# Layer 1 of a two-layer convolution kernel: splines in two partition halves, x1 loaded 64 partitions at a time, output stores ahead of loads

## The chip, the cores and the metric

The kernel runs on one core of a Trainium2 chip. The metric is device time in microseconds (us), the median over runs of the whole kernel. Names of engines: PE is the matrix engine, DVE the vector engine, ACT the scalar engine, POOL the GpSimd engine, SP the engine that issues most of the DMAs.

## What is computed

The input x has 4 images of 16 channels, 256 by 256, in float32. Two layers follow each other, each with a group normalization in front and a residual sum behind:

```python
x = x + L0(group_norm(x))     # 3x3 conv to 16*25 logits, softmax over 25,
                              # weighted sum over the 5x5 neighbourhood
x = x + L1(group_norm(x))     # a KAN convolution, 3x3 neighbourhood
```

The reference adds a third thing to know about layer 1, and it is all that the change touches:

```python
patches = extract_patches(x, k=3, padding=1)
base_w = base_weight.sum(axis=2)
spl_w = (spline_weight * spline_scaler[..., None]).sum(axis=2)
out = einsum('bjhwn,ijn->bihw', silu(patches), base_w)
out = out + einsum('bjhwns,ijns->bihw', b_splines(patches, grid), spl_w)
out = out + bias
```

There are 8 cubic spline bases for each of 16 channels, so 128 spline features of a pixel, one per partition, and beside them the silu of each channel. A padded pixel is zero after normalization: its silu is zero, its splines are those of zero. The residual x of layer 1 is also fed through the matmuls, as an identity weight on the unnormalized x1 rows.

## The kernel before, in words

Layer 0 walks over strips of 32 columns. It writes its result x1 to DRAM buffers `x1s[b]`, one per image, from a store that ACT issues (the very last one POOL issues). Its statistics give, per image, the scale and bias that layer 1 needs (`scales`, L174 on). In the profile layer 0 lasts until about 2039 us, with DVE's reductions at L738 and POOL's products at L906.

Layer 1 walks over 64 units (4 images, 16 units each), a unit being 16 output rows. For unit n:

- `load_x(n, half)` (L984 to L991, the DMA is L988): the unit's x1 rows go to one of three buffers xta, xtb, xtc, each channel repeated over 8 partitions, in two DMAs of 128 partitions by 8 rows (1 MB each).
- `load_tiles(n)` (L995 to L1006, the DMAs are L1003): the same rows once more, 16 channels by 4 row phases d, into the upper 64 partitions of one of three sl buffers, a DMA of 16 neighbouring partitions for each d (128 KB each). Rows outside the image are zeroed by POOL (L999).
- `features(n, between)` (L1025): ACT takes the distance to the knots (L1036, an Abs with scale and bias per partition) over both halves; then for each half (buffers ta, tb) `spline` (L161 to L172) runs ACT steps L164, L166, L167 and DVE steps L168, L169, L170, which write 128 spline rows to the ring. For the second half DVE's `minus_r` (L159) stands in for L166. Between the halves `put` runs: DVE's L1065 adds the bias to the finished psum of unit n-2 and so makes yo.
- `silu(n)` (L1015, the ACT step is L1018) turns the sl rows to silu in the lower 64 partitions; POOL zeroes the outside rows again (L1023).
- `halo(n)`: at image edges POOL copies a pad row into the ring (L1053, L1057); every third unit SP copies two ring rows to the ring's start (L1055).
- `store()` (L1072): two DMAs write yo of unit n-2 to the output.
- `outputs(n)`: PE multiplies the ring rows (L1082) and the sl rows (L1092) by the weights, 48 and 12 matmuls in the program.

Every engine's instructions in layer 1 keep the order of the program text, SP's DMA issues among them; this order is laid down by hand (`in_order`). The loop body (L1127 to L1143) is therefore also SP's queue: halo's copy, then the two x loads of unit n+2, then the two stores of unit n-2, then the four tile loads of unit n+1. A load waits for the last reader of its buffer; a store waits for yo.

The weights are prepared once at the start: `prepare1` (L534) sums the spline weights into `wt` and places the base weights in `ws`; `sel` (L103, L104) spreads a value per channel over 8 partitions each; partition p of the splines stands for channel p // 8 and base p % 8. In `scales`, q holds the silu scale and bias (by p % 16) and the distance scale and bias (by p // 8).

Of the kernel before, what the change touches and what calls it, by code (L numbers as in the profile page):

```python
# [4 lines left out]

# [7 lines left out]
F32 = mybir.dt.float32  # L13
F32R = mybir.dt.float32r
AF = mybir.ActivationFunctionType
# [20 lines left out]
def conv_preact_kernel(  # L36
# [12 lines left out]
    nc = tc.nc  # L49
# [26 lines left out]
    RD = RT + 2  # L76
    RU = 16
    NU = H // RU
    SROWS = (0, 1, 3, 2)
    LAG1 = 2  # L80

    const = ctx.enter_context(tc.tile_pool(name="const", bufs=1))
# [11 lines left out]
    mhalf = const.tile([P, G], F32, name="mhalf")  # L94
    nc.vector.memset(mhalf, -0.5)
    ub = const.tile([P, 1], F32, name="ub")
    ubrow = const.tile([1, C, NS], F32, name="ubrow")
    for s in range(NS):
        nc.vector.memset(ubrow[:, :, s : s + 1], 3.5 - s)
    ident = const.tile([P, P], F32, name="ident")  # L100
    make_identity(nc, ident)

    sel = const.tile([C, C, NS], F32, name="sel")  # L103
    nc.vector.tensor_copy(sel, ident[0:C, 0:C].unsqueeze(2).to_broadcast([C, C, NS]))  # L104
    onec = const.tile([P, 1], F32, name="onec")
    nc.vector.memset(onec, 1.0)
    flag = const.tile([1, 1], mybir.dt.int32, name="flag")
# [15 lines left out]
    ws = const.tile([P, 3, RT, C], F32, name="ws")  # L123
    nc.gpsimd.memset(ws, 0.0)
    for r in range(RT):
        p = P // 2 + SROWS.index(r + 1) * C
        nc.sync.dma_start(ws[p : p + C, 1, r], ident[p : p + C, p : p + C])

    edge = const.tile([P, 5], F32, name="edge")
    stat1 = ctx.enter_context(tc.tile_pool(name="stat1", bufs=1))  # L130
# [43 lines left out]
    def scales(b, psum):  # L174


        def small(n, name):
            return stat1.tile([P, n], F32, name=f"{name}_{b}", tag=f"{name}{b % 2}")

        sums, d, mz, p = small(2 * G, "sums"), small(G, "d"), small(G, "mz"), small(G, "p")  # L180
        q = stat1.tile([P, 6], F32, name=f"q_{b}", tag=f"q{b}")
        nc.vector.tensor_reduce(sums, st1[b].rearrange("p t g k -> p (t g) k"), AX.X, ALU.add)
        yield
        ps = psum()[:, 0 : 2 * G]
        nc.tensor.matmul(ps, lhsT=ones, rhs=sums, start=True, stop=True)
        yield
        part = 1.0 / (GC * CX * NK)
        nc.scalar.activation(d, ps[:, 0:G], AF.Square, scale=part)
        yield

        nc.vector.scalar_tensor_tensor(mz, ps[:, 0:G], part, nrm[b][:, 1], ALU.mult, ALU.subtract)
        nc.vector.scalar_tensor_tensor(d, ps[:, G : 2 * G], part, d, ALU.mult, ALU.subtract)  # L192
        yield
        nc.gpsimd.tensor_add(d, d, nrz[b][:, 1])  # L194
        nc.gpsimd.tensor_tensor(p, d, mhalf, ALU.pow)
        nc.gpsimd.tensor_mul(d, p, nrz[b][:, 0])
        nc.gpsimd.tensor_mul(p, p, gsel_sb)
        nc.gpsimd.tensor_mul(p, p, mz)
        yield
        nc.vector.reduce_sum(q[:, 0:1], d, AX.X)  # L200
        nc.vector.reduce_sum(q[:, 1:2], p, AX.X)
        nc.vector.tensor_scalar(q[:, 1:2], q[:, 1:2], -1.0, None, ALU.mult)
        for k in range(2):
            nc.vector.tensor_scalar(q[:, 2 + k : 3 + k], q[:, k : k + 1], 2.5, None, ALU.mult)
        yield
        ps = psum()[:, 0:2]
        nc.tensor.matmul(
            ps, lhsT=sel.rearrange("p c s -> p (c s)"), rhs=q[0:C, 2:4], start=True, stop=True
        )
        yield  # L210
        nc.vector.tensor_copy(q[:, 4:5], ps[:, 0:1])
        nc.vector.tensor_add(q[:, 5:6], ps[:, 1:2], ub)
        sc[b] = tuple(q[:, k : k + 1] for k in (0, 1, 4, 5))
        yield

    sc = {}
# [31 lines left out]
    def zeros(b, queue):  # L248

        for e in (0, HP - PAD):  # L250
            for r in range(PAD):
                yield partial(
                    queue.dma_start,
                    hs[b][:, e + r].rearrange("s c w -> c s w"),
                    zero[0:C, 0 : NST * SP].rearrange("c (s w) -> c s w", s=NST),
                )
        for h in range(NH):
            for w in (0, (W + 1) * RP):
                yield partial(queue.dma_start, hst[b][h][:, w : w + RP], zero[0:C, 0:RP])
                yield partial(  # L260
                    queue.dma_start,
                    hsl[b][h][:, :, w : w + RP].rearrange("c t r -> (c t) r"), zero[:, 0:RP],
                )
# [178 lines left out]
    with tc.tile_pool(name="prep0", bufs=2) as prep, tc.tile_pool(  # L442
# [42 lines left out]
        for d in range(3):  # L485
# [10 lines left out]

        ups = pstat.tile([P, 1], F32, name="ups", tag="hps")
        nc.tensor.matmul(
            ups, lhsT=ubrow.rearrange("p c s -> p (c s)"), rhs=onec[0:1], start=True, stop=True
        )  # L500
        nc.vector.tensor_copy(ub, ups)
        nc.scalar.activation(edge[:, 0:1], ub, AF.Abs)
# [31 lines left out]
        def prepare1():  # L534

            nc.gpsimd.tensor_mul(sw, sw, ss)
            wc = pre.tile([P, 3, nm], F32, name="wc")
            for d in range(3):
                nc.vector.tensor_reduce(
                    wc[:, d], sw[:, d].rearrange("p k j -> p j k"), AX.X, ALU.add  # L540
                )
            nc.vector.tensor_scalar(wc, wc, -1.0 / 6.0, None, ALU.mult)
            wb1 = pre.tile([nm, nm], F32, name="wb1")
            nc.vector.tensor_reduce(wb1, bw.rearrange("p k j -> p j k"), AX.X, ALU.add)
            for r in range(RT):
                nc.vector.tensor_copy(
                    wt[:, r : r + 3, :, r, :], wc.rearrange("p d (e o) -> p d e o", e=3)
                )
                for d in range(3):
                    p = SROWS.index(r + d) * C  # L550
                    nc.sync.dma_start(
                        ws[p : p + C, :, r, :],
                        wb1[d * C : (d + 1) * C].rearrange("p (e o) -> p e o", e=3),
                    )

# [102 lines left out]
    def layer0(shift):  # L658
# [4 lines left out]
        with tc.tile_pool(name=f"prep{arm}", bufs=2) as prep, tc.tile_pool(  # L663
# [150 lines left out]
            def store(n, xc):  # L814
                b, hf, s = strips[n]
                c0 = s * SW + SW - CX
                v = x1s[b][:, 0 : H * W].rearrange("c (p w) -> p c w", w=W)

                queue = nc.gpsimd if n == len(strips) - 1 else nc.scalar
                queue.dma_start(v[hf * P : (hf + 1) * P, :, c0 : c0 + CX], xc)  # L820
# [110 lines left out]
    def layer1(arm, last, marks, seeds):  # L931
# [5 lines left out]
        with ExitStack() as pools:  # L937
# [27 lines left out]
            def rows(t, dims, r):  # L965

                return bass.AP(tensor=t.tensor, offset=t.offset + r * W, ap=dims)
# [16 lines left out]
            def load_x(n, half):  # L984
                b, u = units[n]
                lo, hs = halves(u)
                a, z = hs[half]
                nc.sync.dma_start(  # L988
                    xtt[n % 3][:, a - lo : z - lo, :],
                    rows(x1s[b], [[CP, C], [0, NS], [1, (z - a) * W]], u * RU - 1 + a),  # L990
                )  # L991

            def load_tiles(n):  # L995
                b, u = units[n]
                t = sl[n % 3][P // 2 :, :, 1 : W + 1]
                for p, q in outside(u):
                    nc.gpsimd.memset(t[p : p + C, q], 0.0)  # L999
                for k, d in enumerate(SROWS):  # L1000
                    q0 = 1 if (u, d) == (0, 0) else 0
                    q1 = RU // RT - (1 if (u, d) == (NU - 1, RD - 1) else 0)
                    nc.sync.dma_start(  # L1003
                        t[k * C : (k + 1) * C, q0:q1, :],
                        rows(x1s[b], [[CP, C], [RT * W, q1 - q0], [1, W]], u * RU - 1 + d + q0 * RT),
                    )  # L1006

            def outside(u):

                return [  # L1010
                    (SROWS.index(d) * C, q)
                    for at, d, q in ((0, 0, 0), (NU - 1, RD - 1, RU // RT - 1)) if u == at
                ]

            def silu(n):  # L1015
                b, u = units[n]
                t = sl[n % 3][0 : P // 2, :, 1 : W + 1]
                nc.scalar.activation(  # L1018
                    t, sl[n % 3][P // 2 :, :, 1 : W + 1], AF.Silu,
                    scale=sc[b][0][P // 2 :], bias=sc[b][1][P // 2 :],  # L1020
                )
                for p, q in outside(u):
                    nc.gpsimd.memset(t[p : p + C, q], 0.0)  # L1023

            def features(n, between):  # L1025
                b, u = units[n]
# [49 lines left out]
            def outputs(n):  # L1076
# [11 lines left out]

                for e in range(3):
                    for t in range(NT):  # L1090
                        v = slice(0, P if e == 1 else P // 2)
                        nc.tensor.matmul(  # L1092
                            yp[t * M : (t + 1) * M],
                            lhsT=ws[v, e].rearrange("p r o -> p (r o)"),
                            rhs=sl[n % 3][v, t : t + NT + 1 : NT, e : e + W],
                            start=False, stop=e == 2,
                        )
                waiting.append((b, u, yp))
# [28 lines left out]
            for n in range(len(units)):  # L1127
                if n % 2:
                    next(more, None)
                if n > 0:  # L1130
                    features(n, put)
                    silu(n)
                    halo(n)
                if n + 2 < len(units):
                    for half in range(2):
                        load_x(n + 2, half)
                store()
                if 0 < n < len(units) - 1:
                    load_tiles(n + 1)
                outputs(n)  # L1140
# [66 lines left out]
```

## Time and profile before

| | us |
|---|---|
| median of 3 runs | 3053.68 |
| the runs | 3051.6 to 3059.32 |
| span of the profiled execution, first to last instruction | 3050.8 |
| DVE busy over the span | 2954.8 (97%) |
| PE busy over the span | 2804.2 (92%) |
| ACT busy over the span | 2252.1 (74%) |
| POOL busy over the span | 1948.5 (64%) |

The three runs are times of the device for the whole kernel; the profiled execution is one more, whose span alone is shown. The busy shares are means over both layers, and the two layers use the engines differently: POOL and PE carry layer 0 along with DVE, while in layer 1 POOL is nearly idle and ACT is full. So layer 1 has to be read from stretches of time after 2087 us. Idle times "before" an instruction are listed with what ended them; the chain of waits follows the end of the program back to what released each step.

### The profile page before, as it was taken

How to read it: one execution, taken by the hardware profiler on the slowest of the kernel's cores; microseconds unless marked ns; L12 is line 12 of the kernel's file. 1: busy time of each engine (PE TensorE's matmuls, PEld its weight loads, DVE VectorE, ACT ScalarE, POOL GpSimd, SP SyncE). 2: the span in 40 equal slices, each digit the busy share in tenths (PEclk: the TensorE clock that was granted, in tenths of full speed). 3: DMA queues.
4: the chain of work that ended last, by engine and by line, in shares of the span. 5: the costliest groups of instructions: out<-in, count | busy, mean ns of one | idle time of the engine just before them, and what ended most of it. 6: DMA issues, size and time to landing. Idle time of an engine off the chain costs nothing.

```text
span 3050.8 us, 39867 instructions
## 1 busy us (share of the span) xinstructions
PE 2804.2 (92%) x14280; PEld 1447.6 (47%) x14280; DVE 2954.8 (97%) x1587; ACT 2252.1 (74%) x2619; POOL 1948.5 (64%) x744
## 2 busy tenths in 40 slices
PE   4699999999989999999999999958999999999998
PEld 3465656656656666666666556632222222222222
DVE  7599999999999999999999999999999999999997
ACT  6566776576765666766645646559999999999996
POOL 4399999999999999999999999980100100000000
PEclk7799999999999999999999999979999999999999
DMA  8988988878978778878857667659999999999993
GB/s 274 254 232 223 261 238 238 230 196 247 244 207 229 201 207 226 241 209 228 234 152 194 179 165 191 162 128 208 201 192 195 195 195 190 199 195 199 192 199 86
DMA packets 353042, 628.40 MB, mean 206 GB/s; under 512 B 41394, under 2 KB 218788, under 8 KB 336964
## 3 DMA queue, kind: packets, MB, share of 16 engines
q1 hardware_dynamic: 320132, 607.39, 81.0%
q10 hardware_dynamic: 30960, 15.73, 1.7%
q8 instruction: 117, 1.92, 0.3%
q0 software_dynamic: 1744, 2.64, 0.3%
q14 instruction: 89, 0.73, 0.1%
HBM read 516.05 MB, written 104.24 MB: 203 GB/s over the span
## 4 chain that ended last, share of the span: by engine, by line
DVE 68%; issue 12%; PE 9%; DMA 5%; ACT 3%; POOL 2%; SPq 1%; DVEq 0%; POOLq 0%; ACTq 0%
DVE nd L738 43%; PE lg L878 6%; DVE ta L169 4%; DVE ta L168 4%; DVE tb L169 4%; DVE tb L168 4%; DVE tb L159 2%; PE lg L882 2%; DVE yo L1065 1%; POOL e L906 1%; DVE r L759 1%; DMA an<-hsl 1%; DVE nd L758 1%; DVE nd L760 1%; DVE lo L396 1%
## 5 line engine op out<-in xcount | busy, mean ns | idle before, releaser
L906 POOL TENSOR_TENSOR e<-e,u 128x1600 f32<-128x1600 f32 x512 | 1788.5, 3543 | 56.4 <-ACT e L901 49.0
L878 PE MATMUL lg<-wm,am 128*128 128x400 f32 x4096 | 1735.7, 505 | 80.3 <-ACT e L901 49.1
L738 DVE TENSOR_REDUCE nd<-e 128x128 f32<-128x3200 f32 x512 | 1749.2, 3478 | 24.3 <-POOL e L906 24.3
L882 PE MATMUL lg<-wn,an 97*128 97x400 f32 x2048 | 1344.3, 656 | 12.8 <-DMA an<-hsl 12.7
L901 ACT ACTIVATE e<-lg 128x800 f32<-128x800 f32 x1024 | 820.0, 837 | 682.8 <-DVE nd L738 440.7
L878 PEld LDWEIGHTS lg<-wm,am 128*128 128x128 f32 x4096 | 759.9, 192 | 400.1 <-ACT e L901 104.5
L1082 PE MATMUL yp<-ring,wt 128*32 128x512 f32 x6144 | 745.3, 597 | 86.6 <-DVE ring L170 62.6
L882 PEld LDWEIGHTS lg<-wn,an 97*128 97x128 f32 x2048 | 388.1, 190 | 330.7 <-issue 21.7
L1082 PEld LDWEIGHTS yp<-ring,wt 128*32 128x32 f32 x6144 | 202.2, 109 | 621.6 <-issue 433.1
L999 POOL MEMSET sl<- 16x256 f32 x6 | 1.8, 306 | 402.9 <-PE yp L1092 396.8
L169 DVE TENSOR_TENSOR ta<-ta,ta 128x2048 f32<-128x2048 f32 (+1 forms) x64 | 147.4, 2303 | 3.0 <-ACT ta L167 2.9
L170 DVE SCALAR_TENSOR_TENSOR ring<-ta,ta 128x2048 f32<-128x2048 f32 (+1 forms) x64 | 147.8, 2310 | 2.5
L786 ACT ACTIVATE z<-xc,nrm 128x256 f32<-128x256 f32 x240 | 144.2, 601 | 6.4 <-POOL xc L766 2.4
L170 DVE SCALAR_TENSOR_TENSOR ring<-tb,tb 128x2048 f32<-128x2048 f32 x64 | 145.6, 2275 | 2.5
L169 DVE TENSOR_TENSOR tb<-tb,tb 128x2048 f32<-128x2048 f32 x64 | 145.2, 2269 | 0.0
L1092 PE MATMUL yp<-sl,ws 64*32 64x512 f32 (+1 forms) x1032 | 131.2, 602 | 0.0
L999 POOL MEMSET slc<- 16x256 f32 x2 | 0.6, 309 | 203.1 <-PE yp L1092 203.0
L167 ACT ACTIVATE ta<-ta 128x2048 f32<-128x2048 f32 (+1 forms) x64 | 123.4, 1928 | 2.0
L194 POOL TENSOR_TENSOR d<-d,nrz 128x8 f32<-128x8 f32 x4 | 2.7, 680 | 189.9 <-DVE d L192 189.9
L167 ACT ACTIVATE tb<-tb 128x2048 f32<-128x2048 f32 x64 | 120.6, 1884 | 0.0
L1018 ACT ACTIVATE sl<-sl,q 64x2048 f32<-64x2048 f32 x43 | 90.0, 2094 | 1.2
L766 POOL TENSOR_TENSOR xc<-xc,nd 128x512 f32<-128x512 f32 x64 | 82.8, 1293 | 8.3 <-DVE nd L760 8.3
(200 smaller groups left out, 2108.8 us busy)
## 6 DMA issues: line engine op xcount, KB each, us to landing
am<-hst SPq DMA_DIRECT2D x512, 194.6 KB
u<-hs SPq DMA_DIRECT2D x320, 288.0 KB
an<-hsl SPq DMA_DIRECT2D x512, 129.8 KB
xta<-x1s SPq DMA_DIRECT2D x40, 1024.0 KB
xtb<-x1s SPq DMA_DIRECT2D x40, 1024.0 KB
xtc<-x1s SPq DMA_DIRECT2D x40, 1024.0 KB
am<-hst SPq DMA_DIRECT2D x256, 129.8 KB
sl<-x1s SPq DMA_DIRECT2D x166, 128.0 KB
```

The source lines that it names most:

```text
L167: nc.scalar.activation(s1, r1, AF.Square, scale=2.0)
L168: nc.vector.scalar_tensor_tensor(s2, t, 2.0, s2, ALU.subtract, ALU.mult)
L169: nc.vector.tensor_mul(s1, s1, r1)
L170: nc.vector.scalar_tensor_tensor(f, s2, 0.0, s1, ALU.min, ALU.subtract if given else ALU.add)
L738: nc.vector.tensor_reduce(nd[:, :, :, j : j + JG].rearrange("p t c j -> p t j c"), e.rearrange("p t j m c d -> p t j c m d"), AX.XY, ALU.add,)
L786: nc.scalar.activation(z, v, f, scale=nrm[b][:, 0, g : g + 1], bias=nrm[b][:, 1, g : g + 1], accum_out=st1[b][:, t, g, columns_of(n) : col ...
L878: nc.tensor.matmul(lg[:, i, :NL], lhsT=am[:, o : o + P], rhs=wm.rearrange("p m c d -> p (m c d)"), start=True, stop=False,)
L882: nc.tensor.matmul(lg[:, i, :NL], lhsT=an[:, o : o + P], rhs=wn.rearrange("p m c d -> p (m c d)"), start=False, stop=True,)
L901: nc.scalar.activation(ev, lg[:, :, :NL], AF.Exp)
L906: nc.gpsimd.tensor_tensor(e[:, 1].rearrange("p j m c d -> p j (m c) d"), e[:, 0].rearrange("p j m c d -> p j (m c) d"), uv, ALU.mult,)
L1082: nc.tensor.matmul(yp[t * M : (t + 1) * M], lhsT=wt[:, d, e].rearrange("p r o -> p (r o)"), rhs=ring[:, r0 + t * RT + d : r0 + t * RT + d ...
L1092: nc.tensor.matmul(yp[t * M : (t + 1) * M], lhsT=ws[v, e].rearrange("p r o -> p (r o)"), rhs=sl[n % 3][v, t : t + NT + 1 : NT, e : e + W], ...
```

## The change

In layer 1 and what feeds it:

- Splines are placed in two partition halves: partition is now half, channel, base within the half (h, c, s with 4 bases each), instead of channel, base. `sel`, `ubrow` and the spline weights (through one matmul with a permutation, `order`) follow.
- `load_x` issues each of its two loads as two DMAs of 64 partitions.
- `load_tiles` puts row phase d of channel c at partition 64 + 4c + d, so one DMA writes every fourth partition of 64. `ws` follows. The scale and bias for silu now come from the same spread as the distance's.
- x1s gets a row of zeros ahead of and behind each image, written by one more DMA per image with the other zeros; tile rows outside the image are then loaded as zeros. POOL's memsets go. To make silu of such a row zero, boundary units run silu in two pieces, the outside row with scale and bias multiplied by zero (`inside`).
- PE's silu matmuls use all 128 partitions for all three column shifts.
- In the loop, `store()` stands ahead of the x loads.

```diff
-    sel = const.tile([C, C, NS], F32, name="sel")
-    nc.vector.tensor_copy(sel, ident[0:C, 0:C].unsqueeze(2).to_broadcast([C, C, NS]))
+    sel = const.tile([C, 2, C, SH], F32, name="sel")
+    for h in range(2):
+        nc.vector.tensor_copy(sel[:, h], ident[0:C, 0:C].unsqueeze(2).to_broadcast([C, C, SH]))
+
+    inside = const.tile([P, 2], F32, name="inside")
+    for k, d in enumerate((0, RD - 1)):
+        nc.vector.reduce_sum(inside[:, k : k + 1], ident[:, d:P:RD], AX.X)
+    nc.vector.tensor_scalar(inside, inside, -1.0, 1.0, ALU.mult, ALU.add)
...
-        nc.vector.tensor_copy(q[:, 4:5], ps[:, 0:1])
-        nc.vector.tensor_add(q[:, 5:6], ps[:, 1:2], ub)
-        sc[b] = tuple(q[:, k : k + 1] for k in (0, 1, 4, 5))
+        nc.vector.tensor_copy(q[:, 4:7], ps[:, 0:3])
+        nc.vector.tensor_add(q[:, 7:8], ps[:, 3:4], ub)
+        for k in range(2):
+            nc.vector.tensor_scalar(
+                q[:, 8 + 2 * k : 10 + 2 * k], ps[:, 0:2], inside[:, k : k + 1], None, ALU.mult
+            )
+        sc[b] = tuple(q[:, k : k + 1] for k in range(4, 12))
...
+        yield partial(
+            queue.dma_start,
+            bass.AP(
+                tensor=x1s[b].tensor, offset=x1s[b].offset,
+                ap=[[CP, C], [(H + 1) * W, 2], [1, W]],
+            ),
+            zero[0 : 2 * C, 0:W],
+        )
...
+            order = pre.tile([P, 2, C, SH], F32, name="order")
+            nc.vector.tensor_copy(order, ident.rearrange("p (c h s) -> p h c s", h=2, s=SH))
+            wcp = ptr0.tile([P, QG, P], F32, name="wcp", tag="tp").rearrange("p g w -> p (g w)")
+            wcp = wcp[:, 0 : 3 * nm]
+            nc.tensor.matmul(
+                wcp, lhsT=order.rearrange("p h c s -> p (h c s)"),
+                rhs=wc.rearrange("p d j -> p (d j)"), start=True, stop=True,
+            )
...
                 a, z = hs[half]
-                nc.sync.dma_start(
-                    xtt[n % 3][:, a - lo : z - lo, :],
-                    rows(x1s[b], [[CP, C], [0, NS], [1, (z - a) * W]], u * RU - 1 + a),
-                )
+                for h in range(2):
+                    nc.sync.dma_start(
+                        xtt[n % 3][h * P // 2 : (h + 1) * P // 2, a - lo : z - lo, :],
+                        rows(x1s[b], [[CP, C], [0, SH], [1, (z - a) * W]], u * RU + a),
+                    )
...
-                t = sl[n % 3][P // 2 :, :, 1 : W + 1]
-                for p, q in outside(u):
-                    nc.gpsimd.memset(t[p : p + C, q], 0.0)
-                for k, d in enumerate(SROWS):
-                    q0 = 1 if (u, d) == (0, 0) else 0
-                    q1 = RU // RT - (1 if (u, d) == (NU - 1, RD - 1) else 0)
+                for d in range(RD):
                     nc.sync.dma_start(
-                        t[k * C : (k + 1) * C, q0:q1, :],
-                        rows(x1s[b], [[CP, C], [RT * W, q1 - q0], [1, W]], u * RU - 1 + d + q0 * RT),
+                        sl[n % 3][P // 2 + d : P : RD, :, 1 : W + 1],
+                        rows(x1s[b], [[CP, C], [RT * W, RU // RT], [1, W]], u * RU + d),
                     )
...
-                t = sl[n % 3][0 : P // 2, :, 1 : W + 1]
-                nc.scalar.activation(
-                    t, sl[n % 3][P // 2 :, :, 1 : W + 1], AF.Silu,
-                    scale=sc[b][0][P // 2 :], bias=sc[b][1][P // 2 :],
-                )
-                for p, q in outside(u):
-                    nc.gpsimd.memset(t[p : p + C, q], 0.0)
+                q0, q1 = 1 if u == 0 else 0, RU // RT - (1 if u == NU - 1 else 0)
+                for a, z, k in ((0, q0, 4), (q0, q1, 0), (q1, RU // RT, 6)):
+                    if a < z:
+                        nc.scalar.activation(
+                            sl[n % 3][0 : P // 2, a:z, 1 : W + 1],
+                            sl[n % 3][P // 2 :, a:z, 1 : W + 1], AF.Silu,
+                            scale=sc[b][k][P // 2 :], bias=sc[b][k + 1][P // 2 :],
+                        )
...
                     for t in range(NT):
-                        v = slice(0, P if e == 1 else P // 2)
                         nc.tensor.matmul(
                             yp[t * M : (t + 1) * M],
-                            lhsT=ws[v, e].rearrange("p r o -> p (r o)"),
-                            rhs=sl[n % 3][v, t : t + NT + 1 : NT, e : e + W],
+                            lhsT=ws[:, e].rearrange("p r o -> p (r o)"),
+                            rhs=sl[n % 3][:, t : t + NT + 1 : NT, e : e + W],
                             start=False, stop=e == 2,
                         )
...
+                store()
                 if n + 2 < len(units):
                     for half in range(2):
                         load_x(n + 2, half)
-                store()
                 if 0 < n < len(units) - 1:
                     load_tiles(n + 1)
```

More of the change, by code (lines that the diff above doesn't have):

```diff
@@ L2 @@
 from functools import partial
-from itertools import chain
 from itertools import chain
@@ L78, in conv_preact_kernel @@
     NU = H // RU
-    SROWS = (0, 1, 3, 2)
     LAG1 = 2
@@ L96, in conv_preact_kernel @@
     ub = const.tile([P, 1], F32, name="ub")
-    ubrow = const.tile([1, C, NS], F32, name="ubrow")
+    SH = NS // 2
+    ubrow = const.tile([1, 2, C, SH], F32, name="ubrow")
     for s in range(NS):
-        nc.vector.memset(ubrow[:, :, s : s + 1], 3.5 - s)
+        nc.vector.memset(ubrow[:, s // SH, :, s % SH : s % SH + 1], 3.5 - s)
     ident = const.tile([P, P], F32, name="ident")
     make_identity(nc, ident)
-    sel = const.tile([C, C, NS], F32, name="sel")
-    nc.vector.tensor_copy(sel, ident[0:C, 0:C].unsqueeze(2).to_broadcast([C, C, NS]))
+    sel = const.tile([C, 2, C, SH], F32, name="sel")
[5 more added lines that the diff above has]
+    nc.vector.tensor_scalar(inside, inside, -1.0, 1.0, ALU.mult, ALU.add)
     onec = const.tile([P, 1], F32, name="onec")
@@ L125, in conv_preact_kernel @@
     for r in range(RT):
-        p = P // 2 + SROWS.index(r + 1) * C
-        nc.sync.dma_start(ws[p : p + C, 1, r], ident[p : p + C, p : p + C])
+        nc.sync.dma_start(ws[P // 2 + r + 1 : P : RD, 1, r], ident[0:C, 0:C])
     edge = const.tile([P, 5], F32, name="edge")
@@ L180, in scales @@
         sums, d, mz, p = small(2 * G, "sums"), small(G, "d"), small(G, "mz"), small(G, "p")
-        q = stat1.tile([P, 6], F32, name=f"q_{b}", tag=f"q{b}")
+        q = stat1.tile([P, 12], F32, name=f"q_{b}", tag=f"q{b}")
         nc.vector.tensor_reduce(sums, st1[b].rearrange("p t g k -> p (t g) k"), AX.X, ALU.add)
@@ L205, in scales @@
         yield
-        ps = psum()[:, 0:2]
+        ps = psum()[:, 0:4]
         nc.tensor.matmul(
-            ps, lhsT=sel.rearrange("p c s -> p (c s)"), rhs=q[0:C, 2:4], start=True, stop=True
+            ps, lhsT=sel.rearrange("p h c s -> p (h c s)"), rhs=q[0:C, 0:4], start=True, stop=True
         )
         yield
-        nc.vector.tensor_copy(q[:, 4:5], ps[:, 0:1])
-        nc.vector.tensor_add(q[:, 5:6], ps[:, 1:2], ub)
-        sc[b] = tuple(q[:, k : k + 1] for k in (0, 1, 4, 5))
+        nc.vector.tensor_copy(q[:, 4:7], ps[:, 0:3])
[5 more added lines that the diff above has]
+        sc[b] = tuple(q[:, k : k + 1] for k in range(4, 12))
         yield
@@ L498, in conv_preact_kernel @@
         nc.tensor.matmul(
-            ups, lhsT=ubrow.rearrange("p c s -> p (c s)"), rhs=onec[0:1], start=True, stop=True
+            ups, lhsT=ubrow.rearrange("p h c s -> p (h c s)"), rhs=onec[0:1],
+            start=True, stop=True,
         )
@@ L546, in prepare1 @@
                 nc.vector.tensor_copy(
-                    wt[:, r : r + 3, :, r, :], wc.rearrange("p d (e o) -> p d e o", e=3)
+                    wt[:, r : r + 3, :, r, :], wcp.rearrange("p (d e o) -> p d e o", d=3, e=3)
                 )
                 for d in range(3):
-                    p = SROWS.index(r + d) * C
                     nc.sync.dma_start(
-                        ws[p : p + C, :, r, :],
+                        ws[r + d : P // 2 : RD, :, r, :],
                         wb1[d * C : (d + 1) * C].rearrange("p (e o) -> p e o", e=3),
@@ L816, in store @@
                 c0 = s * SW + SW - CX
-                v = x1s[b][:, 0 : H * W].rearrange("c (p w) -> p c w", w=W)
+                v = x1s[b][:, W : W + H * W].rearrange("c (p w) -> p c w", w=W)
                 queue = nc.gpsimd if n == len(strips) - 1 else nc.scalar
@@ L1008, in outside @@
[L1008 to L1013, printed above, removed]
+                        sl[n % 3][P // 2 + d : P : RD, :, 1 : W + 1],
+                        rows(x1s[b], [[CP, C], [RT * W, RU // RT], [1, W]], u * RU + d),
+                    )
             def silu(n):
                 b, u = units[n]
-                t = sl[n % 3][0 : P // 2, :, 1 : W + 1]
-                nc.scalar.activation(
-                    t, sl[n % 3][P // 2 :, :, 1 : W + 1], AF.Silu,
-                    scale=sc[b][0][P // 2 :], bias=sc[b][1][P // 2 :],
-                )
-                for p, q in outside(u):
-                    nc.gpsimd.memset(t[p : p + C, q], 0.0)
+                q0, q1 = 1 if u == 0 else 0, RU // RT - (1 if u == NU - 1 else 0)
```

## The prediction

> **What bounds the kernel now.** I read the busy table of the page first, then the busy time of each engine in stretches of layer 1 (from about 2087 us on), then the engines' timelines around one unit, and last the DMA rate in half-microsecond slices. Almost all of the change lies in layer 1. The busy table by stretches has the columns: us, then PE, PE weight load, DVE, ACT and POOL busy with counts, granted clock, DMA share, GB/s.
>
> ```profile
> 2600.00:2800.00 200.00, 190.51 (x1578) 47.26 (x1570) 198.99 (x106) 198.50 (x93) 3.37 (x6) 1.00 0.96 197
> 2800.00:3000.00 200.00, 188.03 (x1560) 47.03 (x1560) 198.89 (x106) 198.46 (x93) 0.31 (x1) 1.00 0.94 195
> ```
>
> DVE and ACT are both 99.4% busy, DMA and PE some 95%. Four resources are nearly tied, so little can be won and any delay is paid. A unit (16 output rows) takes 15.25 us on both DVE and ACT. Now one unit. From the chain of waits (start, length), the yo behind which this unit's silu tiles were issued:
>
> ```profile
> 2595.89 0.75 DVE yo L1065
> ```
>
> From ACT's timeline (start, length), silu of unit xta, then work of the next unit xtb:
>
> ```profile
> 2608.08 2.10 ACT L1018 ACTIVATE sl<-sl,q 64x2048 f32<-64x2048 f32 x1
> 2610.20 3.81 ACT L1036 ACTIVATE xtb<-xtb,q 128x4096 f32<-128x4096 f32 x1
> ...
> 2617.78 1.92 ACT L167 ACTIVATE ta<-ta 128x2048 f32<-128x2048 f32 x1
> ```
>
> From DVE's timeline, unit xtb up to its yo:
>
> ```profile
> 2621.86 2.28 DVE L169 TENSOR_TENSOR ta<-ta,ta 128x2048 f32<-128x2048 f32 x1
> 2624.18 2.29 DVE L170 SCALAR_TENSOR_TENSOR ring<-ta,ta 128x2048 f32<-128x2048 f32 x1
> 2626.39 0.74 DVE L1065 TENSOR_SCALAR yo<-yp,bias_sb 128x512 f32<-128x512 f32 x1
> ```
>
> From SP's timeline of DMA issues:
>
> ```profile
> 2611.91 1.36 SPq L1072 DMA_DIRECT2D out_dram<-yo  x2
> 2613.36 2.75 SPq L1003 DMA_DIRECT2D sl<-x1s  x4
> 2616.22 1.58 SPq L988 DMA_DIRECT2D xta<-x1s  x2
> 2627.16 1.34 SPq L1072 DMA_DIRECT2D out_dram<-yo  x2
> ```
>
> The reader is to see SP's rhythm: it waits for yo (470 us over 54 units in SP's own waits), issues two stores, the four silu tiles for the next unit at once after them, and then, as soon as their buffer is free, the two x1 loads of the unit after next. And a margin: ta's L167 ends at 2619.70, DVE takes it up at 2621.86, so ACT is 2.16 us ahead of need.
>
> **The step that matters: x1 loads between the stores and the silu tiles.** In the old text order SP issues x(n+2), stores, tiles(n+1). The x loads go out early: at 2616.22, as soon as the buffer is free, 11 us before the yo of 2627.13. In the new order all of x(n+2) waits behind the stores, so behind yo of the same unit, and the tiles come last: 2 MB of x now stand ahead of them in the queue. What is queued behind the new wait: four x loads and four tile loads; who waits for the last: silu on ACT, and behind it on ACT the next unit's distance (L1036) and everything DVE needs.
>
> Call X the time from the end of yo to the landing of the tiles. How large may X be? Yo ended at 2596.64 (2595.89 + 0.75). The silu that needs the tiles issued behind it started at 2608.08 and could start 2.16 us later, at 2610.24, without DVE noticing. So X may be 13.6 us. From that silu to the end of yo two units on (2626.39 + 0.74 = 2627.13) is a chain of 16.9 us: silu, distance, L164, L166, L167, then L169, L170, yo. If X is above 13.6, two units last X + 16.9 instead of 30.5. Now X is about 7 (the chain of waits shows the third tile landing at 2603.25, 6.6 after yo).
>
> X after the change is not shown by this trace, so I add it up from rows. The rate of x loads and tile loads stands in the start of layer 1, where tiles(0), x(1) and tiles(1) were queued in one go from 2039.40 (tile issues at 2039.40 and 2042.57, x at 2041.36). Slices of 0.5 us from 2038:
>
> ```profile
> GB/s 0 0 0 0 31 232 229 158 119 139 195 152 123 180 246 246 197 147 246 229 246 246 213 213 180 213 262 246 246 197 94 189 148 109 125 129 129 127 115 10
> ```
>
> First bytes come some 0.7 us after the issue. x (from about 2044 to 2053) runs at about 225 GB/s; the tiles after it (2053 to 2057.5) at about 125, though all DMA engines are busy. So 2.10 MB of x take 9.3 us and 0.52 MB of tiles 4.2 us. After yo: the stores take 1.45 us to issue, x's first bytes come at 2.15; of the stores' 0.26 MB about 0.11 are gone by then (66 to 76 GB/s in the slices after 2627.5). The remaining 0.15 MB and x at 225 GB/s: 10.0 us, to 12.15. Then the tiles. Their rate is one of the unknowns, because the new tiles go to every fourth of 64 partitions instead of 16 neighbours: unchanged it is 4.2 us; at the rate of x, which also spreads its rows over many partitions, 2.3. I take the rate of x, as its spread is the nearer row: X = 14.5. With the old rate it is 16.4. From below: in 2613.0 to 2627.5 stores, tiles and x moved in one unbroken stretch of 14.5 us, 4.2 of it tiles; 10.3 for stores and x, plus 2.3, plus 0.6 to the first byte, is 13.2, under the limit.
>
> The two-unit loop runs from unit 2 to unit 62, 30 times. 14.5 - 13.6 = 0.9 us, 30 times: **+27 us**. At 16.4: +84. At 13.2: nothing.
>
> **The split of x1 into 64 partitions.** Same bytes, four issues of 0.57 us for two, 1.2 us more on SP, which idles 8.7 us a unit now: free. The transfer rate of a 64-partition load is not in the trace. Nearest are the loads of layer 0 onto 32 and 48 partitions (an, am), whose stretches run at 200 to 270 GB/s; the far end is the tiles' 125 GB/s, which would make X about 22 and cost some 260 us. I take 225, unchanged, because the full 128-partition load already goes no faster than those narrow ones. [...]
>
> **The rest, small.** Silu in two pieces in 8 boundary units: by the L167 forms (2304, 2048, 1792 elements: 2130, 1915, 1685 ns) an element costs 0.87 ns; from silu's 2095 the pieces cost 1872 and 536, +0.31 us each; ACT has no idle time to hide it: +2.5 us. Scales: two more DVE instructions of 0.15 us a batch, and the weights' reordering at the start (one 128x128 copy, one matmul, small reductions): +1 us together, nothing if they fall in waits, 2 at most. The 16 POOL memsets (0.3 us) that go: nothing, POOL is idle in layer 1; PE's silu matmuls on 128 rows instead of 64 take 604 for 601 ns, and PE waits anyway; if PE had no cover it would be 3 us. Four zero stores to x1s lie beside layer 0's DVE work. The new zero rows spare nothing on the path. The compiled order of the changed program lets a DMA on SP wait for the one eight places before it; with ten a unit the third and fourth tile wait for the stores' landing, some 4 to 7 us after yo (6.63 in the chain): x still fills the queue then, so nothing. The ring copies (0.26 MB, one unit in three) enter the queue just ahead of the stores and may lift X there by up to a microsecond; that stays in the range.
>
> The start of layer 1 keeps its path: x of unit 2 is issued at 2062.94 behind the last x1 store and lands at 2075.84; faster tiles don't move that. The 35 us of PE work after the last DVE step stay.
>
> Sum: 27 + 2.5 + 1 = 30.5 on the span of 3050.8, so 3081. The fastest run shown is 3051.6, the median 3053.68, 2.9 above the span: **3084**.
>
> **Rivals.** (1) The tiles still arrive in time: X stays under 13.8. The stores occupy the queue thinly, x streams beside them, and everything packs as in the unbroken stretch above. For it: that stretch gives 13.2; DMA then has less work than now, because tiles go faster. Against it: x's first byte can't come before 2.15 us after yo. Time 3050 to 3060, no change; the gain is at most the DVE waits at the start (3.23 + 0.72 + 1.45 us behind x of unit 2) and the 5 us that DVE idles from 2087 to 3000, so 3043 if x ran faster too. It decides as soon as X is 13.6 or less. (2) Loads lose: the tiles gain nothing from the spread, or halves load slower. X 15.5 to 17.5, 3114 to 3175. For it: tiles run at 125 now; against: the narrow loads of layer 0. (3) Halves much slower, DMA becomes the bound: above 3175.
>
> **How the numbers follow.** Forecast case, X 13.8 to 15.5: 0.43, 3063 to 3114. Rival 1: 0.32, of which 0.05 faster. Rival 2: 0.22. Rival 3: 0.03. The range 3047 to 3140 takes in case 1 nearly whole, the forecast, and the nearer half of rival 2, some 0.82. Faster than 0.3% (9 us, about what a measurement of this kernel can tell) 0.05, within 0.27, slower 0.68.
>
> **What would show it.** Right: ACT idle before L1018 in most units, put down to the DMA of sl, some 0.5 us a unit; the same idle time on DVE before L169 of ta behind ACT; SP order stores, four x, four tiles; tiles landing 14 to 15 us after yo; DMA share lower than 0.95. Wrong: DVE still 99.4% busy with a unit of 15.25 us (rival 1), or idle time before the distance (L1036) on x's DMA rather than before silu (rival 3). Tile slices near 125 GB/s speak for rival 2.

## The result, and the profile after

The changed kernel takes 3163.88 us (median of 4 runs, 3161.09 to 3168.04), the kernel before 3052.64 beside it: 1.0369 times as long, 95% interval 1.0351 to 1.0387. The direction was right, the size was not: 111 us instead of 30, and outside the stated range.

First the stretches of layer 1 in the profile after (us, then PE, PE weight load, DVE, ACT and POOL busy with counts, granted clock, DMA share, GB/s):

```profile
2600.00:2800.00 200.00, 164.37 (x1396) 46.07 (x1392) 180.40 (x94) 177.50 (x85) 0.00 (x0) 0.92 0.79 169
2800.00:3000.00 200.00, 165.11 (x1372) 46.52 (x1368) 178.60 (x94) 179.41 (x85) 0.80 (x2) 0.90 0.81 176
```

PE, DVE and ACT have become less busy, DMA with them (0.96 to 0.80). Nothing is full any more, so the time is lost in a chain of waits and not in work. The waits from 2087 to 3120 us (us in total, times, longest) name it:

```profile
ACT sl L1031 <- DMA sl<-x1s: 74.9, 35, 4.8
DVE ta L173 <- ACT ta L171: 59.5, 48, 1.6
ACT slc L1031 <- DMA slc<-x1s: 37.5, 15, 4.5
DVE ta L172 <- ACT ta L168: 20.9, 30, 0.9
```

ACT waits 112 us in 50 waits before silu (L1031, formerly L1018) for the silu tiles; before there was no such wait. DVE then waits for ACT. Layer 0 is as it was: in 500 to 2000 us DVE is busy 1489.8 us, formerly 1493.0. Now four units. SP's issues of the changed kernel:

```profile
2885.18 1.35 SPq L1084 DMA_DIRECT2D out_dram<-yo  x2
2886.64 2.48 SPq L1013 DMA_DIRECT2D xtc<-x1s  x4
2889.22 2.48 SPq L1021 DMA_DIRECT2D sl<-x1s  x4
...
2900.51 1.66 SPq L1084 DMA_DIRECT2D out_dram<-yo  x2
...
2919.31 1.34 SPq L1084 DMA_DIRECT2D out_dram<-yo  x2
```

ACT's silu in the same stretch, with the idle time before it and its releaser:

```profile
2902.35 2.09 ACT L1031 ACTIVATE sl<-sl,q 64x2048 f32<-64x2048 f32 x1 [3.99 <-DMA sl<-x1s]
...
2917.60 2.09 ACT L1031 ACTIVATE slc<-slc,q 64x2048 f32<-64x2048 f32 x1
```

And DVE's yo:

```profile
2884.41 0.74 DVE L1077 TENSOR_SCALAR yo<-yp,bias_sb 128x512 f32<-128x512 f32 x1
2899.74 0.74 DVE L1077 TENSOR_SCALAR yo<-yp,bias_sb 128x512 f32<-128x512 f32 x1
2918.54 0.74 DVE L1077 TENSOR_SCALAR yo<-yp,bias_sb 128x512 f32<-128x512 f32 x1
2933.87 0.74 DVE L1077 TENSOR_SCALAR yo<-yp,bias_sb 128x512 f32<-128x512 f32 x1
```

The loop can be read off. Yo ends at 2885.15; stores, four x loads and four tile loads go out behind it; silu starts on the tiles at 2902.35, 17.2 us later; the yo two units on ends at 2919.28, 16.9 us after silu started. Two units take 34.13 us (2884.41 to 2918.54) instead of 30.5. The units alternate here, 15.3 and 18.8, since one wait serves two units; elsewhere two shorter waits share the loss, which is why there are 50 waits for 30 loops. Over the 50 waits the time from the end of yo to silu is 17.15 us in the mean (15.8 to 18.3), 3.55 above the limit of 13.6: 30 loops of 3.55 us are 106 of the 111 us.

### The profile page after: what moved, and what is told of

Same layout as the page of the kernel before. It is cut to its first block, busy times and chain, and to the rows that moved or that the text cites. A ratio compares the mean times of both kernels' runs of the same rounds, so it can differ in the third digit from the quotient of the medians.

```text
span 3166.3 us, 40049 instructions
## 1 busy us (share of the span) xinstructions
PE 2799.0 (88%) x14282; PEld 1482.1 (47%) x14282; DVE 2967.2 (94%) x1600; ACT 2257.4 (71%) x2627; POOL 1953.3 (62%) x729
## 4 chain that ended last, share of the span: by engine, by line
DVE 47%; ACT 14%; DMA 13%; PE 10%; issue 8%; SPq 5%; POOL 3%; ACTq 0%; POOLq 0%; DVEq 0%
DVE nd L762 37%; PE lg L902 6%; DMA sl<-x1s 5%; DVE ta L173 3%; ACT ta L171 2%; ACT ta L168 2%; POOL e L930 2%; ACT ta L170 2%; ACT xtc L1048 2%; PE lg L906 2%; SPq L1013 1%; ACT xta L1048 1%; ACT e L925 1%; SPq L1021 1%; PE yp L1094 1%
## 5 line engine op out<-in xcount | busy, mean ns | idle before, releaser
L906 PE MATMUL lg<-wn,an 97*128 97x400 f32 x2048 | 1347.0, 658 | 16.6 <-DMA an<-hsl 16.4
L1094 PE MATMUL yp<-ring,wt 128*32 128x512 f32 x6144 | 810.9, 646 | 208.9 <-DVE ring L174 184.8
L1094 PEld LDWEIGHTS yp<-ring,wt 128*32 128x32 f32 x6144 | 219.0, 117 | 750.3 <-issue 490.9
L1103 PE MATMUL yp<-sl,ws 128*32 128x512 f32 x1032 | 153.4, 591 | 0.0
L1031 ACT ACTIVATE sl<-sl,q 64x2048 f32<-64x2048 f32 (+2 forms) x49 | 91.7, 1883 | 75.2 <-DMA sl<-x1s 74.9
L1048 ACT ACTIVATE xtb<-xtb,q 128x4096 f32<-128x4096 f32 (+2 forms) x21 | 79.9, 3804 | 7.6 <-DMA xtb<-x1s 7.0
```

The costliest lines, as they stand in the source:

```text
L906: nc.tensor.matmul(lg[:, i, :NL], lhsT=an[:, o : o + P], rhs=wn.rearrange("p m c d -> p (m c d)"), start=False, stop=True,)
L1048: nc.scalar.activation(t, t, AF.Abs, scale=sc[b][2], bias=sc[b][3])
L1094: nc.tensor.matmul(yp[t * M : (t + 1) * M], lhsT=wt[:, d, e].rearrange("p r o -> p (r o)"), rhs=ring[:, r0 + t * RT + d : r0 + t * RT + d ...
L1103: nc.tensor.matmul(yp[t * M : (t + 1) * M], lhsT=ws[:, e].rearrange("p r o -> p (r o)"), rhs=sl[n % 3][:, t : t + NT + 1 : NT, e : e + W], ...
```

## The experiments

All times are medians; ratios are to the kernel before, run beside them. The theory: the tiles stand behind yo and behind 2 MB of x, and land past the limit of 13.6 us after yo. The rivals are these: x in halves of 64 partitions, or the new tile layout, moves more slowly; or the silu pieces and the start cost the time.

**The old order with everything else of the change, and the new order alone.**

```diff
+                if n + 2 < len(units):
+                    for half in range(2):
+                        load_x(n + 2, half)
                 store()
-                if n + 2 < len(units):
-                    for half in range(2):
-                        load_x(n + 2, half)
```

> The changed kernel with the one line moved back: x loads of unit n+2 ahead of the stores, all else of the change kept (halves, strided tiles, zero rows). Theory A (the tiles wait behind yo and behind 2 MB of x): the loss goes, 3048 to 3060 us, the tiles land some 6 us after yo, and ACT does not idle before silu. Rival B (64-partition halves move x slower, or the new tile layout does): most of the loss stays, 3110 to 3165 us. Rival C (silu in pieces, scales, the start): a loss of 10 us or more stays, with idle time spread over boundary units.

Measured 3053.51 us, ratio 1.0012 [1.0001, 1.0023]. A stretch of layer 1:

```profile
2600.00:2800.00 200.00, 182.67 (x1584) 51.47 (x1576) 199.00 (x106) 198.50 (x95) 2.12 (x2) 0.95 0.82 197
```

DVE and ACT are as full as in the kernel before, at the same pace and the same GB/s, while the DMA share is 0.82 instead of 0.96. So in the old order neither the halves nor the strided tiles cost time, and the lower DMA share is of no use to anything. All parts of the change but the order together cost 3 us (0.3 to 7 by the interval).

The reverse, the kernel before with its loads behind the stores (`store()` moved ahead of the x loads as in the change, and nothing else):

> The kernel before with that one line moved: stores ahead of the x loads, nothing else of the change. Theory A: x and tiles now wait behind yo; the loss appears here too. The changed kernel has 17 us from yo to the tiles (two units of 34 us); with the old tile layout, 4.2 us of tiles instead of 3.7, that is 17.5, and 30 times (17.5 - 13.6) is 117 us: 3160 to 3180 us. Rivals B and C: 3050 to 3065 us.

Measured 3174.36 us, 1.0397 [1.0375, 1.0419]. One moved line makes the whole loss. It is larger than the whole change's. One of its loops, yo on DVE and silu on ACT:

```profile
2608.12 0.74 DVE L1065 TENSOR_SCALAR yo<-yp,bias_sb 128x512 f32<-128x512 f32 x1
2626.91 2.09 ACT L1018 ACTIVATE sl<-sl,q 64x2048 f32<-64x2048 f32 x1 [5.05 <-DMA sl<-x1s]
```

From yo's end at 2608.86 to silu it takes 18.05 us; over all its waits the mean is 17.8, against 17.15 in the changed kernel.

**Tiles ahead of x, both behind yo.**

```diff
                 store()
+                if 0 < n < len(units) - 1:
+                    load_tiles(n + 1)
                 if n + 2 < len(units):
                     for half in range(2):
                         load_x(n + 2, half)
-                if 0 < n < len(units) - 1:
-                    load_tiles(n + 1)
```

> The changed kernel with SP's order stores, tiles, x: everything still behind yo, but the tiles ahead of the 2 MB. Theory A: the tiles land some 7 us after yo and silu does not wait. x of unit n+2 then lands 15 to 16.5 us after yo, and its limit is 13.6 + 2.1 = 15.7 (the distance starts one silu later): 3050 to 3080 us, with what is lost as idle time before the distance. Rival B: 3110 us or more. If being behind yo alone cost the time, whatever the order after it, 3140 us or more.

Measured 3090.61 us, 1.0129 [1.0110, 1.0147]: most of the loss goes, and the rest is 10 us above the expectation. ACT's waits from 2120 to 3000 us:

```profile
ACT xtc L1048 <- DMA xtc<-x1s: 12.4, 12, 2.0
ACT xta L1048 <- DMA xta<-x1s: 10.9, 10, 1.9
ACT xtb L1048 <- DMA xtb<-x1s: 9.3, 10, 2.1
```

The wait has moved from silu to the distance (L1048), as foreseen: x is now last in the queue. From yo to the distance it takes 16.9 us in the mean of the whole layer's 36 waits (16.1 to 17.9; one of the longer ones runs from 2608.44 to 2625.75), where 15 to 16.5 were expected and 15.7 allowed: 30 times 1.2 us and the 3 us of the rest make 39 of the 40 us that this kernel loses. The shortfall has the sign of the prediction's: the waiting engine starts later than the bytes I count allow.

**Stores out of SP's way.** Here the stores go out from POOL (`nc.gpsimd.dma_start` for `nc.sync.dma_start` in `store`), and SP issues x and tiles without waiting for yo.

> The changed kernel with the two output stores issued from POOL instead of SP; SP's order is x, then tiles, none of it behind yo. Theory A: x goes out when its buffer is free, some 13 us before yo, the tiles behind it land some 3 us after yo, and silu does not wait: 3050 to 3060 us, up to 3085 if POOL's work for the stores slows DVE as POOL's pad copies do (2.5 us for 2.2 us). If only the tiles' place behind x mattered and not the wait for yo, the loss would stay: 3140 us or more. Rival B: 3110 us or more.

Measured 3055.90 us, 1.0016 [1.0005, 1.0026]. The tiles still stand behind x in SP's queue, and all but 5 us of the loss is gone: the place behind x alone does little harm, it is harmful behind yo. For the slowing of DVE by POOL that the expectation allows for, the trace of before has in layer 1 (from 2087 us on) a single step, 2.49 us beside a pad copy (L169 at 2307.31) where the median is 2.28; beside the five pad copies after it DVE's steps are within 0.01 us of their medians.

**The stores last** (x, tiles, stores on SP):

> The changed kernel with SP's order x, tiles, stores: neither loads nor tiles behind yo of their unit. Theory A: the same time as with x, stores, tiles, since DVE and ACT are full there: 3046 to 3060 us; the tiles only land earlier. If tiles landing earlier were worth something, it would be below 3046.

Measured 3053.63 us, 1.0002 [0.9986, 1.0019]. Earlier tiles are worth nothing that shows once they are in time.

**The limit moved instead of the transfers.**

```diff
-                    if k == 1:
+                    if k == 0:
                         between()
```

> The changed kernel with its new order on SP kept, but yo made ahead of the first spline half instead of between the halves, some 6.8 us earlier in the unit on DVE (three instructions of 2.2 to 2.3 us). This moves the limit, not the transfers: from yo to the tiles it still takes 17 us, but silu asks for them 20.4 us after yo instead of 13.6. Theory A (a loop of two units, yo to tiles to silu to yo): no idle time before silu, 3048 to 3062 us. Rival (silu waits for the tiles since DMA has too little room in a unit, whatever the loop): 3150 us or more. What could spoil it: the psum of unit n-2 must be ready earlier; if PE is not done, DVE idles before yo and not ACT before silu.

Measured 3051.07 us, 0.9999 [0.9984, 1.0014]. This keeps the new order, the halves, the strided tiles and the same bytes behind each yo. A stretch of layer 1, then SP's lines, and yo on DVE and silu on ACT:

```profile
2600.00:2800.00 200.00, 179.27 (x1584) 50.40 (x1576) 199.06 (x106) 198.50 (x94) 4.49 (x2) 0.97 0.91 196
```

```profile
2604.58 1.35 SPq L1084 DMA_DIRECT2D out_dram<-yo  x2
2606.03 2.48 SPq L1013 DMA_DIRECT2D xtc<-x1s  x4
2608.61 2.47 SPq L1021 DMA_DIRECT2D sl<-x1s  x4
2619.84 1.35 SPq L1084 DMA_DIRECT2D out_dram<-yo  x2
```

```profile
2603.81 0.75 DVE L1077 TENSOR_SCALAR yo<-yp,bias_sb 128x512 f32<-128x512 f32 x1
2624.06 2.09 ACT L1031 ACTIVATE sl<-sl,q 64x2048 f32<-64x2048 f32 x1
```

The same queue in the same order; stores follow each other at 15.26 us; silu starts 19.5 us after yo's end at 2604.56 and finds its tiles there, without a wait. So it is the loop from yo over the tiles to silu and back, not too much traffic.

**The price of each transfer in the loop.** Four kernels leave out transfers of the changed kernel; what is not loaded keeps old data, the computing stays. With 30 loops, a fall of 30 us is 1 us of the time from yo to the tiles. The kernel before took 3049.99 us beside these four and 3052.64 beside the changed kernel, so a fall is good to some 3 us.

```diff
-                for h in range(2):
+                for h in range(2 if n < 3 or u == 0 else 1):
                     nc.sync.dma_start(
                         xtt[n % 3][h * P // 2 : (h + 1) * P // 2, a - lo : z - lo, :],
```

> The changed kernel, which loads only the lower 64 partitions of x (one of the two halves, 1.05 MB instead of 2.10) in all units but the first three and each image's first; the upper half keeps old data, so half of the splines are computed from old rows. All computing stays. Theory A by bytes: the time from yo to the tiles falls from 16.9 us by 4.7 (1.05 MB at 225 GB/s) to 12.2, under the limit of 13.6: 3050 to 3062 us, no idle time before silu but after the few full loads. Rival (the loss comes from the wait for yo with a fixed latency, whatever the bytes behind it): 3150 us or more.

Measured 3070.24 us, 1.0065 [1.0048, 1.0081], 8 above the expectation. Its ACT waits from 2120 to 3000 us:

```profile
ACT sl L1031 <- DMA sl<-x1s: 12.1, 3, 6.0
ACT slc L1031 <- DMA slc<-x1s: 6.1, 2, 5.6
```

Five waits are left. Three of them, of 6.0, 5.9 and 5.6 us, make 17.4 of the 18.2 us: they are those of the tiles that stand behind the full x of an image's first unit. I had put these units at next to nothing. Behind half of x two waits are left, of 0.5 and 0.2 us.

With the condition `2 if n < 3 or u == 0 or half == 0 else 1`:

> The same, but only the second row half leaves out its upper 64 partitions: 1.57 MB of x in those units. Theory A by bytes: 16.9 - 2.3 = 14.6 us from yo to the tiles, 1.0 over the limit, 30 loops: 3075 to 3095 us. Rival (fixed latency): 3150 us or more.

Measured 3092.34 us, 1.0144 [1.0127, 1.0161]: 71.5 us less than the changed kernel, 2.4 us a loop for 0.52 MB, 220 GB/s; or 2.65 us and some 200 GB/s, if the three loops with an image's first unit, which still load x in full, are left out of the count.

With `for d in range(RD if n < 3 else 2)` in `load_tiles`:

> The changed kernel, which loads only two of the four row phases of the silu tiles in all units but the first three; the others keep old rows, so silu and the residual are computed from old data there. The trace of the changed kernel shows 4.1 us of tile bytes behind x. If tiles cost that, X falls by 2.0 to 14.9: 3085 to 3100 us. If they moved at x's 225 GB/s as I had predicted and the rest was latency, it falls by 1.2 only: 3110 to 3125 us.

Measured 3122.71 us, 1.0244 [1.0227, 1.0261]: 41 us less, 1.4 us a loop for 0.26 MB, some 190 GB/s. This is the second of the two expectations. All the tiles' bytes then cost 2.7 us of the 4 that the slices (below) show.

With `for g in range(1)` in `store`:

> The changed kernel, which writes only one of the two output stores of each unit (half of the output stays unwritten). x is then issued 0.66 us earlier and 0.13 MB less lies ahead (0.58 us at 225 GB/s): X falls by some 1.2 to 15.7, 3110 to 3130 us. If the stores stand beside x without delaying it, only the issue counts: 3135 to 3150 us.

Measured 3131.82 us, 1.0266 [1.0249, 1.0283]: 32 us less, 1.1 us a loop, near the 1.2 expected and a little over the stated 3130.

## Why the prediction was wrong

The mechanism, its place, its limit and its number of loops were right; the time X from yo to the tiles was mis-sized, in two of its terms: the tiles behind x, and the time from their last bytes to the start of silu.

- **The limit, 13.6 us, and the chain of 16.9 us:** right. The trace after shows 16.9 from silu's start to the end of yo two units on, and the kernel with yo made earlier shows that the limit decides.
- **X = 14.5 us:** the step that failed. It is 17.15 in the mean. At 30 loops a microsecond is 30 us, so an error of 2.65 is 80 us. Take the loop from the yo that ended at 2625.85 to its silu, 16.9 us. Half-microsecond slices from 2630 us show its end (x behind that yo, then its tiles); the digits are the busy share of the DMA engines in each slice, in tenths:

```profile
2625.10 0.74 DVE L1077 TENSOR_SCALAR yo<-yp,bias_sb 128x512 f32<-128x512 f32 x1
2642.78 2.10 ACT L1031 ACTIVATE sl<-sl,q 64x2048 f32<-64x2048 f32 x1 [0.36 <-DMA sl<-x1s]
DMA  9989999999999999799997400000000444986978
GB/s 311 180 213 246 262 213 197 246 262 213 213 197 246 262 197 191 141 178 195 193 191 123 82 18 0 0 0 0 0 0 20 92 166 131 307 184 246 295 180 229
```

- x runs at some 230 GB/s to about 2637.5, 11.7 us after yo; predicted 12.15. (By a count of the bytes it ends some 0.6 us later, at about 2638.1, since x and tiles overlap there, with 13 packets of 1 KB among 10 of x in 2637.5 to 2638.0; the tiles then take 3.4 us and not 4.) This term was right, and the kernel with three quarters of x comes out at 200 to 220.
- The tiles last to about 2641.5, 4 us instead of 2.3. By the kernel with half the tiles their bytes are 2.7 of it. The other 1.3 us do not go with their bytes. In the two slices from 2640.5 the DMA engines are 0.7 and 0.4 busy and move 123 and 82 GB/s; what makes up that time no run here shows.
- From the last bytes to silu's start at 2642.78 it takes 1.2 us (0.8 to 1.3, as close as the slices tell); I had counted nothing. What that time is made of stays open.
- The trace of before held a warning, the issue of x of unit 2 on SP and its landing in the chain of waits:

```profile
2062.94 1.16 SPq L988 DMA_DIRECT2D xtc<-x1s  x2
2063.50 12.34 DMA xtc<-x1s
```

Nothing stood ahead of it in the queue, though two more x loads were issued behind it from 2064.14. Its first bytes show in the slice from 2064.0, and it landed at 2075.84. That is 12.9 us, where 0.7 to the first byte and 9.3 at the rate make 10.0. I quoted the landing for another purpose and priced x by its rate. With these 2.9 us more the sum is 17.4. This agrees with the measured X in total and not term by term, for behind yo x itself took what its rate says; that it comes so near is partly luck.
- **Range and chances:** I bounded X by changing one term at a time (the tiles' rate gave 16.4) and left out that the time from bytes to landing was missing from every case, the bounds too. The measured time lies in the span of rival 2 (the tiles gain nothing, or halves load slower), but its cause is not what happened. In the slices behind yo the tiles run at some 170 to 185 GB/s in the changed kernel and some 155 to 165 in the kernel before with stores first, and x at some 230 in both, in halves and whole. That the halves would lose nothing was right, on a weak ground: the stretches of layer 0 that I read it from also hold the loads of u, so their rate was not that of the narrow loads alone.
- **The rest, 3.5 us:** right as a sum; the old order with all the rest is 3.0 us above before, 0.3 to 7 by the interval. The silu pieces, extra DVE steps, POOL's memsets and the issues on SP are in that, and no run takes them apart.
- **Rival 1**, the tiles in time: it fell, for silu waits for them 50 times. They are in time only where the order or the place of yo was changed again.

## What to carry to other kernels

Where two or three engines are tied at 99%, look for loops that pass through a queue: from an event on one engine, over everything queued behind the instruction that waits for it, to the engine that needs the last of it, and back. Price the loop by measured landings, issue to use, and not by average rates; its loss is (loop time - units in it x time of a unit) x number of loops, and each microsecond missed is paid that often. What helped here: the store that waits for a result behind the loads that wait for nothing, or on another queue, or its result made earlier.

## What the runs showed that I had not expected

- A tile DMA onto every fourth partition took longer to issue on SP here than one onto 16 neighbouring partitions: 593 against 422 ns in the old order (the old order with the rest of the change, and before), 598 against 533 in the new (the changed kernel, and before with stores first; all medians). Its bytes moved faster, at some 170 to 185 against 155 to 165 GB/s behind yo.
- The same traffic at the same pace shows a DMA share of 0.96 with the old tile layout and whole loads, 0.82 with strided tiles and halves (both in the old order; with these and yo earlier it is 0.91). A DMA share near one was no proof that DMA set the pace: lowering it by 0.14 moved the time by 3 us, upwards.
- The granted clock of PE is 0.99 to 1.00 in layer 1 before and 0.90 to 0.92 after. The moved line alone brings it to 0.91 to 0.93; all the rest of the change without it to 0.95 to 0.97, at the old pace, so that there it cost nothing that shows.
